# Window attention on TensorE: one head per tile of the array, and one score tile for a pair of windows

## The chip, the cores and the metric

The kernel runs on one NeuronCore of a Trainium2 chip, as a single launch. The metric is the device time of that launch in microseconds; the core's own time is the kernel's time. The kernel before takes 12572.97 us, the median of three runs (12561.93, 12572.97 and 12574.42).

## What is computed

A network of four layers works on images `x` of 4 x 256 x 64 x 64 (batch, channels, rows, columns), in fp32. Each layer adds to `x` what it makes of its group-normalised input. Layers 0 and 1 are attention layers, layers 2 and 3 are Mamba layers (a recurrence along 4096 positions); the change touches the attention layers alone. In such a layer, for each of the 4 images:

- `y` comes from a gated recurrence along one axis, after four 1x1 convolutions with tanh and sigmoid.
- `y` is cut into 8 x 8 windows of 64 positions. `q`, `k` and `v` are linear in `y` (256 to 3 x 256).
- For each window, the mean `q` is compared with the mean `k` of all 64 windows, and the 4 best windows are chosen.
- The window's 64 queries attend to the 4 x 64 = 256 positions of the chosen windows, in 8 heads of 32 channels:

```python
attn = softmax(einsum('bphqd,bphkd->bphqk', qh * SCALE, kh))
out = einsum('bphqk,bphkd->bphqd', attn, vh)
```

- `out` plus a depthwise 3x3 convolution of `v` ("lepe" in the code) goes through a last linear map `wo`.

## The kernel before

For each batch the kernel does layer 0, layer 1, layer 2 and layer 3 one after the other. `attention_layers` does both attention layers of a batch; its order of work is written out by hand, so each engine executes its instructions in the order of the source, and only waits on semaphores shift them against the other engines. A tile that is allocated again under the same tag waits for those that used the buffer before; `bufs` says how many buffers a tag has.

A layer has two phases. `scan_phase` goes over 8 strips of 8 columns and produces `y`, the keys and values (written to DRAM by window, `kvd`) and the value image `vimg`. `window_phase` then goes over 32 pairs of windows, `for i in range(n_pair)` (L620 on), and is software-pipelined: iteration `i` issues the scores, least values and exponentials of pair `i + 1` and the transposes and values of pair `i`. The steps:

- `gather` (L455 on): loads the keys and values of the four chosen windows into `kv`, 128 rows for two of the chosen windows and two such halves (`j`) along the free axis.
- `queries` (L257 on): two 1x1 convolutions per strip make `q` for 8 windows; ScalarE writes it to `qbuf` (L266), and two DMAs copy each half of it to the other 64 partitions (`double`, L275). `qbuf` holds two heads beside each other, `[P, 2, NW, 2, 64]`, and has zeros where a row belongs to the other head; they are written once, at the start of the program (L105).
- `scores` (L480): for each of the two windows `w`, a matmul has 64 rows (two heads of 32 channels), 128 columns (two heads x 64 queries, block diagonal because of the zeros) and 128 key positions. Row half `r` holds different keys. That is 16 matmuls per pair. The result is `sc[w]`, a PSUM tile of 128 x 1024 for each window, with two buffers.
- `smallest` (L491): VectorE reduces `sc[w]` to the least value of each query and head, once for each window (the scores carry the opposite sign, so this is the softmax's maximum).
- `exps` (L502): ScalarE takes the exponentials, 4 instructions of 128 x 256 per window, each with the sum of its rows; it issues them in halves, `(0, 1)` and `(2, 3)`, around the copies of `turned`.
- `normalise`: VectorE takes the reciprocal of the sums (L512), and POOL multiplies (L514, 128 x 1024).
- `turn` (L528): TensorE transposes the attention weights, 8 transposes per window; `turned` copies them to SBUF, half by VectorE (L539) and half by ScalarE (L541).
- `values` (L552): 8 matmuls per window with 128 rows (key positions), 64 columns (the channels of two heads) and 128 moving columns (the queries of both heads). Half of what they write belongs to the wrong head. The result is `ov`, one buffer.
- `own_rows` (L565): VectorE adds the four useful quarters of `ov` to `vimg`, 32 partitions each.

Between these, the loop runs a convolution per pair in most iterations (`queries` for a later strip or `project`, the map `wo` of an earlier one, both L208; `add` at L577 is the sum that follows the latter), `taps` on POOL (the depthwise convolution of the last two strips, L229, L230 and L242), and the steps of the next group norm, planned in `mids` (after the first `smallest`) and `ends` (at the end of an iteration): sums L149, means L155, centring L157, squares L165, sums of squares L169.

fp32 matmuls appear in the trace as two instructions each, so that the 16 matmuls of a pair's scores are 32 rows of L480; transposes appear as one.

Of the kernel before, what the change touches and what calls it, by code (L numbers as in the profile page):

```python
# [24 lines left out]
NH = 4  # L25
# [20 lines left out]
class Net:  # L46
# [33 lines left out]
    def attention_layers(self, x, w_drams, v_drams):  # L80
        tc, nc = self.tc, self.nc
        with ExitStack() as ctx:
# [17 lines left out]
                [big.tile([P, 2, NW, 2, 64], F32, name=f"q{i}{m}") for m in range(2)]  # L100
                for i in range(2)
            ]
            for t in qbuf[0] + qbuf[1]:
                for r in range(0, P, 32):
                    nc.gpsimd.memset(t[r : r + 32, :, :, 1 - r // 32 % 2, :], 0.0)  # L105
# [151 lines left out]
            def queries(lay, s, m, psum):  # L257
# [4 lines left out]
                def evict():  # L262
                    for h in range(NH):
                        rows = slice(h * 32, h * 32 + 32)
                        b, h2 = divmod(h, 2)
                        nc.scalar.activation(  # L266
                            q[rows, b, :, h2, :].rearrange("p w (j i) -> p w j i", i=8),
# [166 lines left out]
            def window_phase(lay, work, psum, idx, nxt):  # L434
# [31 lines left out]
                sc = {}  # L466
# [3 lines left out]
                def scores(i):  # L470
                    sj, a = divmod(i, 4)
                    for w in range(2 if i < n_pair else 0):
                        sc[w] = psum.tile([P, 2, 4, P], F32, tag="sc", name="sc", bufs=2)
                        t = kv[i, w]
                        for cq in range(4):
                            m, b = divmod(cq, 2)
                            for r in range(2):
                                rows = slice(r * 64, r * 64 + 64)
                                k0 = b * P + m * 64
                                nc.tensor.matmul(  # L480
                                    sc[w][:, r, cq, :],
                                    qbuf[sj % 2][m][rows, b, 2 * a + w].rearrange("p h t -> p (h t)"),
                                    t[rows, :, k0 : k0 + 64], start=True, stop=True,
                                )

                mn = {}

                def smallest(i, w):
                    if i < n_pair:
                        mn[w] = self.small.tile([P, 4], F32, tag="mn", name="mn", bufs=4)  # L490
                        nc.vector.tensor_reduce(  # L491
                            mn[w], sc[w].rearrange("p r c n -> p c r n"), AX.XY, ALU.min
                        )

                def exps(i, w, part=range(4)):
                    if i < n_pair:
# [4 lines left out]
                        for cq in part:  # L501
                            nc.scalar.activation(  # L502
# [1494 lines left out]
```

## Time and profile before

| | us |
|---|---|
| median of three runs | 12572.97 |
| the profiled execution, its own time | 12578.04 |
| span of its instructions | 12576.3 |
| busy in the span: PE / DVE / POOL / ACT | 10378.1 / 10244.0 / 9022.1 / 7241.3 |
| L480 scores, matmuls (8192 rows), union of their times | 575.6 |
| L552 values, matmuls (8192 rows), union of their times | 595.9 |
| L491 least values (512) | 610.0 |
| L565 own rows (1024, 418 ns each) | about 428 |
| L266 queries to SBUF (512, median 680 ns each) | about 348 |
| first scores to last values, first window phase | 226.7 to 509.0 |
| first scores to last values, second window phase | 709.5 to 1006.2 |

How to read it: the profile is one execution. "Busy" is the time in which an engine has work in flight; matmuls overlap each other, so a matmul's own duration (289 ns for L480) is longer than the distance to the next one. The name in front of a line number is the engine; `x2048` is a count; the shapes are partitions x elements. After the bar stand the busy time, the mean of one in ns, and the time the engine sat idle before such instructions, with what ended it. In a timeline the first number is the start in us, the second the length of a run of like instructions. The mean granted clock of TensorE over the span is 0.915 of full speed.

### The profile page before, as it was taken

The page shows a single profiled execution, that of the slowest core. Times are in us where ns is not written, and L with a number is a line of the kernel's source. Part 1 is how long each engine was busy: PE and PEld are TensorE (multiplying, and loading weights), DVE is VectorE, ACT ScalarE, POOL GpSimd, SP SyncE. Part 2 cuts the span into 40 slices and gives each one's busy share as a digit, 9 for nine tenths or more (in the row PEclk, how much of TensorE's full clock was granted, in tenths as well). Part 3 has the DMA queues.
Part 4 walks back from the last instruction along what each step waited for, and adds up shares of the span by engine and source line. Part 5 has one row for each costly group of instructions (what it writes and reads, how often), then busy time and mean ns, then how long its engine had stood idle before and what let it go on. Part 6 is the DMA issues. An engine that isn't in the chain of part 4 may idle for free. (4 is left out here: it accounts for less than half of the span.)

```text
span 12576.3 us, 159645 instructions
## 1 busy us (share of the span) xinstructions
PE 10378.1 (83%) x54656; PEld 6079.4 (48%) x54656; DVE 10244.0 (81%) x9074; ACT 7241.3 (58%) x13292; POOL 9022.1 (72%) x4634
## 2 busy tenths in 40 slices
PE   8987887777898788778789878877778987887787
PEld 4664444443466454444446645444434664444443
DVE  6778997887677899798767789978976778997897
ACT  4565554776456555477646655547764565554776
POOL 4666886887466688688746668868874666886887
PEclk9998998998899899899889989989988998998998
DMA  3343444554334455455433445445543344554554
GB/s 96 106 130 129 171 168 137 168 169 141 98 107 126 132 169 169 137 170 169 141 98 108 127 133 170 168 137 169 169 141 97 107 128 131 171 168 138 169 168 142
DMA packets 687147, 1782.94 MB, mean 142 GB/s; under 512 B 89856, under 2 KB 197888, under 8 KB 685312
## 3 DMA queue, kind: packets, MB, share of 16 engines
q1 hardware_dynamic: 686336, 1772.74, 43.6%
q8 instruction: 435, 7.13, 0.2%
q14 instruction: 376, 3.08, 0.1%
HBM read 1610.91 MB, written 94.37 MB: 136 GB/s over the span
## 5 line engine op out<-in xcount | busy, mean ns | idle before, releaser
L925 POOL TENSOR_TENSOR hc<-h,cb 128x1024 f32<-128x1024 f32 x2056 | 4817.5, 2351 | 1099.0 <-DVE h L919 502.8
L919 DVE TENSOR_TENSOR_SCAN h<-da,m_state,pb 128x1024 f32<-128x1024 f32 x1248 | 2920.4, 2340 | 162.0 <-DVE pb L913 1.9
L872 PE MATMUL y<-ident,hc 128*128 128x128 f32 x16384 | 2378.0, 294 | 313.7 <-POOL hc L925 211.4
L872 PEld LDWEIGHTS y<-ident,hc 128*128 128x128 f32 x16384 | 2098.8, 152 | 979.4 <-POOL hc L925 374.5
L913 DVE TENSOR_TENSOR pb<-du,pb 128x1024 f32<-128x1024 f32 x1672 | 2025.8, 1212 | 147.3 <-PE pb L844 98.8
L856 ACT ACTIVATE da<-delta,m_v 128x1024 f32<-128x1024 f32 x1672 | 1899.1, 1141 | 215.9 <-DVE h L919 205.4
L844 PE MATMUL pb<-m_parts,pick 128*128 128x512 bf16 x3280 | 1082.2, 414 | 896.9 <-DVE h L919 893.7
L502 ACT ACTIVATE pr<-sc,mn 128x256 f32<-128x256 f32 x2048 | 956.7, 478 | 783.9 <-PE pt_ps L528 560.7
L514 POOL TENSOR_TENSOR pr<-pr,sm 128x1024 f32<-128x1024 f32 x512 | 967.8, 1896 | 572.3 <-DVE sm L512 392.4
L844 PEld LDWEIGHTS <-pick 128*128 128x128 bf16 x3280 | 253.0, 101 | 1884.2 <-DVE h L919 1226.5
L919 DVE TENSOR_TENSOR_SCAN h<-da,pb 128x1024 f32<-128x1024 f32 x424 | 969.7, 2287 | 55.5 <-DVE pb L913 1.4
L830 POOL TENSOR_TENSOR bb<-du,bb 128x1024 f32<-128x1024 f32 x376 | 888.7, 2363 | 71.8 <-DMA bb<-m_cd 65.2
L491 DVE TENSOR_REDUCE mn<-sc 128x4 f32<-128x1024 f32 x512 | 610.0, 1219 | 257.4 <-PE sc L480 256.0
L919 DVE TENSOR_TENSOR_SCAN h<-dap,m_state,bb 128x1024 f32<-128x1024 f32 x288 | 672.1, 2334 | 80.4 <-ACT dap L856 67.7
L528 PE MATMUL pt_ps<-ident,pr 128*128 128x128 f32 x4096 | 572.3, 283 | 144.5 <-ACT pts L541 64.2
L208 PE MATMUL conv_ps<-att_y,att_wb 128*128 128x512 f32 x1536 | 688.8, 593 | 0.0
L856 ACT ACTIVATE dap<-delta,m_v 128x1024 f32<-128x1024 f32 x376 | 419.6, 1116 | 457.7 <-DVE h L919 349.1
L552 PE MATMUL ov_ps<-pts,kv 128*64 128x128 f32 x8192 | 595.9, 294 | 91.1 <-DVE vimg L565 74.6
L480 PE MATMUL sc<-kv,q 64*128 64x128 f32 x8192 | 575.6, 289 | 81.4 <-DMA kv<-kv_dram 58.6
L528 PEld LDWEIGHTS pt_ps<-ident,pr 128*128 128x128 f32 x4096 | 466.5, 144 | 314.1 <-issue 152.2
L480 PEld LDWEIGHTS sc<-kv,q 64*128 64x128 f32 x8192 | 518.3, 197 | 124.6 <-issue 46.5
L552 PEld LDWEIGHTS ov_ps<-pts,kv 128*64 128x64 f32 x8192 | 468.1, 144 | 216.3 <-DVE vimg L565 131.1
(263 smaller groups left out, 18265.0 us busy)
## 6 DMA issues: line engine op xcount, KB each, us to landing
cb<-m_cd SPq DMA_DIRECT2D x2048, 512.0 KB, 3.8
kv<-kv_dram SPq DMA_DIRECT2D x2048, 128.0 KB, 2.6
bb<-m_cd SPq DMA_DIRECT2D x376, 512.0 KB, 5.1
q<-q SPq DMA_DIRECT2D x256, 256.0 KB, 3.9
kv_dram<-kst SPq DMA_DIRECT2D x128, 256.0 KB, 3.5
kv_dram<-vn SPq DMA_DIRECT2D x128, 256.0 KB, 3.6
x<-in_x_dram SPq DMA_DIRECT2D x8, 2048.0 KB, 10.7
m_pe<-in_pe_dram SPq DMA_DIRECT2D x32, 512.0 KB, 5.2
```

The costliest lines, as they stand in the source:

```text
L480: nc.tensor.matmul(sc[w][:, r, cq, :], qbuf[sj % 2][m][rows, b, 2 * a + w].rearrange("p h t -> p (h t)"), t[rows, :, k0 : k0 + 64], start= ...
L502: nc.scalar.activation(t[:, cq].rearrange("p j r t -> p r j t"), sc[w][:, :, cq, :].rearrange("p r (j t) -> p r j t", j=2), AF.Exp, bias=m ...
L514: nc.gpsimd.tensor_tensor(t, t, s.rearrange("p (a o) -> p a o", o=1).to_broadcast([P, 4, 256]), ALU.mult,)
L528: nc.tensor.transpose(pt[w][j][:, cq, :], t[:, cq, j].rearrange("p r t -> p (r t)"), self.ident,)
L552: nc.tensor.matmul(ov[i][b * 64 : b * 64 + 64, m, :, :, w, :], t[:, j, c0 : c0 + 64], pts[w][j][:, cq, :], start=(j == 0), stop=(j == 1),)
L830: nc.gpsimd.tensor_tensor(pb[i], slots[i][0]["du"], pb[i], ALU.mult)
L844: nc.tensor.matmul(pb[i][:, ss], self.pick[:, n : n + 1].to_broadcast([P, P]), blk["parts"][:, ss], start=True, stop=True,)
L856: nc.scalar.activation(da[i], blk["delta"], AF.Exp, scale=blk["a"](n))
L872: nc.tensor.matmul(blk["y"][:, ss], t[:, ss], self.ident, is_transpose=True, start=(n == 0 and ss.start % NT == 0), stop=(n == DS - 1 and ...
L913: nc.vector.tensor_tensor(pb[i], blk["du"], pb[i], ALU.mult)
L919: nc.vector.tensor_tensor_scan(h[i][:, ss], da[i][:, ss], pb[i][:, ss], state, ALU.mult, ALU.add)
L925: nc.gpsimd.tensor_tensor(hc[i][:, ss], h[i][:, ss], cb[i][:, ss], ALU.mult)
```

## The change

The array is used in smaller tiles, one head per matmul.

- `qbuf` loses the axis with two heads, and the zeroing at the start goes. `evict` writes 64 partitions in one instruction, 2 instructions in place of 4.
- `scores` has 32 rows (one head) and 64 columns (its queries) per matmul: 32 matmuls per pair in place of 16, on 8 tiles of the array (4 row positions x 2 column positions). Both windows go to one PSUM tile `sc[i]` of 128 x 2048, with one buffer.
- `smallest` reduces both windows at once.
- `exps` reads its parts at other places of `sc[i]`; number and shape stay.
- `values` has 32 columns (one head's channels) and 64 moving columns: 32 matmuls per pair in place of 16, on 4 column tiles. `ov` is half as large.
- `own_rows` becomes one instruction on 128 partitions.
- In the loop, one `smallest(i + 1)` follows `scores(i + 1)`; the second call, which came after `turn(i, 0)` and `mids`, is gone.

```diff
-                [big.tile([P, 2, NW, 2, 64], F32, name=f"q{i}{m}") for m in range(2)]
+                [big.tile([P, 2, NW, 64], F32, name=f"q{i}{m}") for m in range(2)]
                 for i in range(2)
             ]
-            for t in qbuf[0] + qbuf[1]:
-                for r in range(0, P, 32):
-                    nc.gpsimd.memset(t[r : r + 32, :, :, 1 - r // 32 % 2, :], 0.0)
...
                 def evict():
-                    for h in range(NH):
-                        rows = slice(h * 32, h * 32 + 32)
-                        b, h2 = divmod(h, 2)
+                    for b in range(2):
+                        rows = slice(b * 64, b * 64 + 64)
                         nc.scalar.activation(
-                            q[rows, b, :, h2, :].rearrange("p w (j i) -> p w j i", i=8),
+                            q[rows, b].rearrange("p w (j i) -> p w j i", i=8),
...
                 def scores(i):
                     sj, a = divmod(i, 4)
-                    for w in range(2 if i < n_pair else 0):
-                        sc[w] = psum.tile([P, 2, 4, P], F32, tag="sc", name="sc", bufs=2)
-                        t = kv[i, w]
-                        for cq in range(4):
-                            m, b = divmod(cq, 2)
-                            for r in range(2):
-                                rows = slice(r * 64, r * 64 + 64)
-                                k0 = b * P + m * 64
-                                nc.tensor.matmul(
-                                    sc[w][:, r, cq, :],
-                                    qbuf[sj % 2][m][rows, b, 2 * a + w].rearrange("p h t -> p (h t)"),
-                                    t[rows, :, k0 : k0 + 64], start=True, stop=True,
-                                )
...
                     if i < n_pair:
+                        sc[i] = psum.tile([P, 2, 2, 2, 2, P], F32, tag="sc", name="sc", bufs=1)
+                        for w in range(2):
+                            for m in range(2):
+                                for r in range(2):
+                                    for h in range(2):
+                                        r0 = r * 64 + h * 32
+                                        rows = slice(r0, r0 + 32)
+                                        for b in range(2):
+                                            k0 = b * P + m * 64
+                                            nc.tensor.matmul(
+                                                sc[i][b * 64 : b * 64 + 64, r, h, w, m, :],
+                                                qbuf[sj % 2][m][rows, b, 2 * a + w],
+                                                kv[i, w][rows, :, k0 : k0 + 64],
+                                                start=True, stop=True,
+                                            )
...
+                def smallest(i):
+                    if i < n_pair:
+                        mn[i] = self.small.tile([P, 8], F32, tag="mn", name="mn", bufs=4)
                         nc.vector.tensor_reduce(
-                            mn[w], sc[w].rearrange("p r c n -> p c r n"), AX.XY, ALU.min
+                            mn[i].rearrange("p (g h) -> p g h", h=2),
+                            sc[i].rearrange("p r h w m n -> p (w m) h r n"), AX.XY, ALU.min,
                         )
...
                         for cq in part:
+                            m, h = divmod(cq, 2)
                             nc.scalar.activation(
                                 t[:, cq].rearrange("p j r t -> p r j t"),
-                                sc[w][:, :, cq, :].rearrange("p r (j t) -> p r j t", j=2),
-                                AF.Exp, bias=mn[w][:, cq : cq + 1], scale=-1.0,
+                                sc[i][:, :, h, w, m, :].rearrange("p r (j t) -> p r j t", j=2),
+                                AF.Exp, bias=mn[i][:, w * 4 + cq : w * 4 + cq + 1], scale=-1.0,
...
                 def values(i, w):
                     if w == 0:
-                        ov[i] = psum.tile([P, 2, 2, 8, 2, 8], F32, tag="ov", name="ov_ps", bufs=1)
+                        ov[i] = psum.tile([P, 2, 8, 2, 8], F32, tag="ov", name="ov_ps", bufs=1)
...
                             for b in range(2):
-                                cq = 2 * m + b
-                                c0 = C + cq * 64
-                                nc.tensor.matmul(
-                                    ov[i][b * 64 : b * 64 + 64, m, :, :, w, :],
-                                    t[:, j, c0 : c0 + 64], pts[w][j][:, cq, :],
-                                    start=(j == 0), stop=(j == 1),
-                                )
+                                for h in range(2):
+                                    p0 = b * 64 + h * 32
+                                    c0 = C + m * P + p0
+                                    nc.tensor.matmul(
+                                        ov[i][p0 : p0 + 32, m, :, w, :], t[:, j, c0 : c0 + 32],
+                                        pts[w][j][:, 2 * m + h, b * 64 : b * 64 + 64],
+                                        start=(j == 0), stop=(j == 1),
+                                    )
...
-                        for r in range(4):
-                            rows = slice(r * 32, r * 32 + 32)
-                            out = vimg[rows, :, 8 * sj : 8 * sj + 8, 1 + a * 16 : 17 + a * 16]
-                            nc.vector.tensor_tensor(
-                                out, ov[i][rows, :, r % 2].rearrange("p m j w i -> p m j (w i)"),
-                                out, ALU.add,
-                            )
-                        del ov[i]
+                        out = vimg[:, :, 8 * sj : 8 * sj + 8, 1 + a * 16 : 17 + a * 16]
+                        nc.vector.tensor_tensor(
+                            out, ov.pop(i).rearrange("p m j w i -> p m j (w i)"), out, ALU.add
+                        )
...
                 scores(0)
+                smallest(0)
                 for w in range(2):
-                    smallest(0, w)
                     exps(0, w)
                     normalise(0, w)
...
                     scores(i + 1)
-                    smallest(i + 1, 0)
+                    smallest(i + 1)
                     for t in mids.get(i, ()):
                         t()
                     turn(i, 0)
-                    smallest(i + 1, 1)
                     exps(i + 1, 0, (0, 1))
```

More of the change, by code (lines that the diff above doesn't have):

```diff
@@ L24 @@
 NW = 8
-NH = 4
 TOPK = 4
@@ L464, in gather @@
                                 )
[L466 removed]
+                sc, mn = {}, {}
                 def scores(i):
                     sj, a = divmod(i, 4)
[L472 to L484 removed]
@@ L486, in window_phase @@
-                mn = {}
-                def smallest(i, w):
-                    if i < n_pair:
-                        mn[w] = self.small.tile([P, 4], F32, tag="mn", name="mn", bufs=4)
+                    if i < n_pair:
+                        sc[i] = psum.tile([P, 2, 2, 2, 2, P], F32, tag="sc", name="sc", bufs=1)
[13 more added lines that the diff above has]
+                                            )
```

## The prediction

> **What bounds the kernel now.** I read the page first, for the share of each engine and the groups that the diff touches:
>
> ```profile
> PE 10378.1 (83%) x54656; PEld 6079.4 (48%) x54656; DVE 10244.0 (81%) x9074; ACT 7241.3 (58%) x13292; POOL 9022.1 (72%) x4634
> ...
> L502 ACT ACTIVATE pr<-sc,mn 128x256 f32<-128x256 f32 x2048 | 956.7, 478 | 783.9 <-PE pt_ps L528 560.7
> L514 POOL TENSOR_TENSOR pr<-pr,sm 128x1024 f32<-128x1024 f32 x512 | 967.8, 1896 | 572.3 <-DVE sm L512 392.4
> ...
> L491 DVE TENSOR_REDUCE mn<-sc 128x4 f32<-128x1024 f32 x512 | 610.0, 1219 | 257.4 <-PE sc L480 256.0
> ...
> L552 PE MATMUL ov_ps<-pts,kv 128*64 128x128 f32 x8192 | 595.9, 294 | 91.1 <-DVE vimg L565 74.6
> L480 PE MATMUL sc<-kv,q 64*128 64x128 f32 x8192 | 575.6, 289 | 81.4 <-DMA kv<-kv_dram 58.6
> ```
>
> The shares average over the whole network and the chain that ended last lies in the later layers, so neither decides. The counts do: L502 runs 8 times per pair of windows, so there are 256 pairs, 32 in each of 8 window phases (4 batches x 2 layers). From the first score to the last value they last 282 to 286 us in the first layer and 297 in the second, some 2,320 of 12,576 us. Nothing outside them changes by more than a few us.
>
> Then the timeline of one pair in mid-phase (start, length, engine, line):
>
> ```profile
> 407.80 2.75 ACT L266 ACTIVATE q<-conv_ps,neg_bq 32x512 f32<-32x512 f32 x4
> 407.88 2.06 PE L480 MATMUL sc<-kv,q 64*128 64x128 f32 x32
> ...
> 409.09 2.35 DVE L491 TENSOR_REDUCE mn<-sc 128x4 f32<-128x1024 f32 x2 [0.87 <-PE sc L480]
> ...
> 409.86 1.09 PE L528 MATMUL pt_ps<-ident,pr 128*128 128x128 f32 x8
> ...
> 410.79 1.88 PE L208 MATMUL conv_ps<-att_y,att_wb 128*128 128x512 f32 x4
> 411.04 0.47 ACT L502 ACTIVATE pr<-sc,mn 128x256 f32<-128x256 f32 x1 [0.49 <-PE pt_ps L528]
> ...
> 411.96 1.71 DVE L565 TENSOR_TENSOR vimg<-ov_ps,vimg 32x256 f32<-32x256 f32 x4
> ...
> 413.72 2.35 PE L552 MATMUL ov_ps<-pts,kv 128*64 128x128 f32 x32 [0.17 <-DVE vimg L565]
> ...
> 415.48 0.49 ACT L502 ACTIVATE pr<-sc,mn 128x256 f32<-128x256 f32 x1
> 415.84 0.22 ACT L502 ACTIVATION_READ_ACCUMULATOR pr<-sc,mn 128x1 f32 x1
> 415.93 2.75 ACT L266 ACTIVATE q<-conv_ps,neg_bq 32x512 f32<-32x512 f32 x4
> 416.00 1.86 PEld L480 LDWEIGHTS sc<-kv,q 64*128 64x128 f32 x32 [0.17 <-issue]
> ```
>
> L480 returns every 8.12 us, and TensorE is occupied nearly throughout: **PE's own order of work sets the pair.** The last `exp` of the pair ends at 416.06, after the next scores have begun; two `sc` tiles let them overlap.
>
> **What the change does to this chain.** Scores, least value and `exp`s of a pair now share one `sc` tile (`bufs=1`, as large as the two before). Scores of the next pair can't start before ScalarE has read the last `exp` of this one. That closes a loop over three engines, in which none works ahead. Its terms:
>
> 1. Last accumulator read to first weight load: 0.05 (51 ns where L480 waited for ScalarE now).
> 2. Scores. The trace doesn't show eight tiles at once. Now the 16 instructions of one window run on two row tiles in eight rounds of 112 ns, the two starts of a round 7 ns apart, 1.16 from first load to last end. After: 64 instructions on eight tiles (4 row x 2 column), again eight per tile. Eight tiles 7 ns apart add 0.04; 64-column loads (L552) have rounds of 109. I take 1.15. Below 1.12 it can't go: that is one tile's own eight. The upper bound is the present pace, a load and a matmul per 56 ns: 64 x 0.056 + 0.27 = 3.85. I choose the low end, since in each round two matmuls already start 7 ns apart and the third waits for its own tile.
> 3. PE to VectorE: 0.05.
> 4. One reduction of 2048 elements: 128x512 takes 0.67 (L308), 128x1024 1.22, so two more steps of 0.55: 2.30 (bounds 2.2 and the two it replaces, 2.36).
> 5. VectorE to ScalarE: 0.10.
> 6. Eight `exp`s and two copies: a block of exp-exp-copy-exp-exp starts 2.30 after the one before where nothing holds it (747.06 to 749.36), and ends 2.42 after its start: 4.72. The held block today starts at 413.64 because the second turn ends at 413.55; in the loop that turn ends 2.31 after the first `exp`, so it holds nothing.
>
> Sum 0.05+1.15+0.05+2.30+0.10+4.72 = **8.37 us, against 8.12: +0.25 per steady pair.** So the quicker matmuls are paid for by the lost overlap.
>
> A rule weighed. Row: two tiles' matmuls start 7 ns apart. The Trainium skill, TensorEngine Tiling (Array Packing), section Performance Considerations, Instruction Overhead, puts about 60 cycles on every matmul and warns against tiling a dimension that is already small. At the 2.4 GHz that its page TensorE: Matmul & The Clock Gate gives in its head table, that is 25 ns; 64 would take 1.6 us, an estimate from these two pages, and the loop would be 8.8. The 7 ns of this trace speak against it for different tiles, but only for two.
>
> **What else changes inside the pair.** It all falls off the path:
> - Values: 64 instructions, half as many columns, four column tiles instead of two. By the same rounds 0.7 us per window with its tail, now about 1.1. Bounds: 0.5, and 32 x 0.056 + 0.27 = 2.1. They end about 8.1 into the loop, under the last `exp`s; with the upper bound they would add about 1.
> - L565: four operations of 0.42 on 32 partitions become one on 128. ScalarE's 32x512 (0.68) and 128x512 (0.69) show that partitions cost nothing, so 0.42. It saves VectorE 1.3 per pair, which had kept values waiting ([0.17 <-DVE vimg]); the late thing there becomes the copies of the turned tiles.
> - L266: four of 0.68 become two; 1.38 saved, hidden under scores and reduction. The q copies move half the bytes, three pairs ahead of use. The 15.7 us of zeroing at the start end 1.0 after VectorE's mean is ready: -1.0 once.
> - POOL needs 2 x 1.89 + 4/3 x 2.83 = 7.55 per pair, with a 2.47 every fourth pair of the second layer 8.2: still under 8.37, but with little room.
>
> **Pairs that stall today gain.** In the second layer every fourth pair takes 11 to 12.3 us. Its cause:
>
> ```profile
> 834.51 1.23 DVE L491 TENSOR_REDUCE mn<-sc 128x4 f32<-128x1024 f32 x1 [0.88 <-PE sc L480]
> 837.16 1.22 DVE L169 TENSOR_REDUCE gn_s<-att_xn 128x4 f32<-128x1024 f32 x1 [1.43 <-ACT att_xn L165]
> 838.30 1.21 DVE L491 TENSOR_REDUCE mn<-sc 128x4 f32<-128x1024 f32 x1
> ```
>
> The statistics' reduction stands between the two least values and waits for a square that waits for the 2.75 eviction; everything behind is late, and PE drops to half clock for 3.4 us. After, one L491 goes ahead of it and the eviction is half as long. What is late next is the first copy (1.14 behind the reduction), then the second block by 0.6: 8.97.
>
> **The sum for one batch** (start-to-start intervals of L480, from the timeline):
> - 22 steady pairs of the first layer and 10 of the second, +0.25 each: +8.0.
> - The other 17 intervals of the second layer: 158.2 now. After: five with the reduction 8.97, five beside them with column sums 8.6, two where two taps and the 2.47 meet on POOL 10.25, five 8.6 to 8.4: 150.9. -7.3.
> - Last five intervals of the first layer, 47.0, bound by POOL's queue: -1.2.
> - Phase start: both windows' scores before the first `exp`, which pushes eight taps of VectorE (8.3 us) and the next L491 back: +1.0 each, +2.0. The third interval is 7.86 now, no convolution in it, 8.37 after: +1.0 for two. Pairs without convolution leave PE 2 us idle and may meet half clock (0.5 granted at 258.5 today): +1.0.
> - Tails: -0.3 and, with L565 between values and the last projection, -2.5: -2.8.
> - Four evictions fewer beside each of two strips in the scan phase: -1.0.
>
> 8.0-7.3-1.2+2.0+1.0+1.0-2.8-1.0 = -0.3; four batches -1.2, zeroing -1.0: **-2 us.** The profiled execution took 12578.0 (span 12576.3), 5 above the median, so 12578 - 2 stands for a median of 12571. Its own error: 0.15 per steady pair (32 x 4 x 0.15 = 19), as much for the stalled ones, 12 for starts: about 40.
>
> **Rivals.**
> 1. *The tiles don't run eight at a time* (slower). Place: term 2, decisive from about 1.5 us on. If four overlap, 16 rounds make it 2.05, +0.9 per pair, x 248 = +223: 12,795. At the present pace +2.7, +670: 13,240. Half clock in a third of the pairs would add 1 to those, +80: 12,650. For it: no more than two tiles are ever shown together, and PE is emptier. Against: the 7 ns, and that PE is still busy some 6 us of 8.4.
> 2. *The waits are finer than the tile* (faster). If the first window's scores start as soon as its own `exp`s are through, about half of term 2 leaves the loop: 7.8 per pair, 0.55 x 46 x 4 = 100 less: 12,470. Against: today the second window's first load waits for ScalarE as a whole tile would; and both windows now lie interleaved in one tile.
> 3. *It doesn't do what it says*: a reduction through strides or eviction over 64 partitions slower than its row. 0.3 on term 4 is +75: 12,645.
>
> **How the numbers follow.** Forecast 55%, of which 0.15 below, 0.27 within and 0.13 above 0.2% (25 us, about what a measurement of this kernel can tell from no change). Rival 1 20%, slower; rival 3 8%, slower or same; rival 2 17%, faster. Faster 0.15 + 0.17 = 0.32, same 0.27 + 0.02 = 0.29, slower 0.39. The forecast's own range is 12,530 to 12,610; the given one, 12,470 to 12,700, leaves out four overlapping tiles and worse, and little below.
>
> **What would show it.** Right: L480 starts 0.05 after L502's last read in nearly every steady pair, its run is 1.15, L491 x256 takes 2.30, L565 x256 0.42, the period is 8.37, and PE's idle time before L480 is put down to L502. Wrong: an L480 run above 1.5 (rival 1), L480 starting before L502 has ended (rival 2), L491 above 2.4 (rival 3), or a granted clock in the window phases clearly below the 0.94 to 0.96 of now. If the period is right and the total is not, the stalled pairs were mis-sized.

## The result, and the profile after

The changed kernel takes 12635.21 us (median of 5 runs, 12622.74 to 12641.08), the kernel before 12572.97 (5 runs on the same chip): a ratio of 1.0051, 95% interval 1.0040 to 1.0062. So it is 0.5% slower, about 62 us, where the forecast was 2 us less. The profiled execution took 12630.46 us; its span is 52.4 us longer than that of the profile before.

The page of the changed kernel, head and groups (busy time, mean of one in ns, idle time before them and its main releaser):

```profile
span 12628.7 us, 191060 instructions
...
PE 10051.6 (80%) x71040; PEld 5667.3 (45%) x71040; DVE 9883.3 (78%) x8050; ACT 7057.2 (56%) x13036; POOL 8962.5 (71%) x4570
...
L502 ACT ACTIVATE pr<-sc,mn 128x256 f32<-128x256 f32 x2048 | 954.3, 478 | 995.6 <-DVE mn L489 678.1
L514 POOL TENSOR_TENSOR pr<-pr,sm 128x1024 f32<-128x1024 f32 x512 | 968.2, 1896 | 632.9 <-DVE sm L512 356.6
L489 DVE TENSOR_REDUCE mn<-sc 128x8 f32<-128x2048 f32 x256 | 586.6, 2291 | 285.1 <-PE sc L478 284.8
L554 PE MATMUL ov_ps<-pts,kv 128*32 128x64 f32 x16384 | 400.7, 235 | 183.7 <-ACT pts L541 95.6
L478 PE MATMUL sc<-kv,q 32*64 32x128 f32 x16384 | 365.6, 298 | 186.2 <-ACT pr L502 107.7
```

Every engine is busy for less time than before, PE by 327 us, and the kernel is slower. The right-hand column says why: scores now wait for ScalarE's exponentials (L478, released by `pr` L502), the reduction waits for the scores (L489, by `sc`), and the exponentials wait for the reduction (L502, by `mn` L489: 678 us; before, most of that idle time was put down to the turned tile, `pt_ps`). That is a ring of waits, each engine idle while another works.

One pair of the changed kernel in the timeline (start, length, engine, line):

```profile
407.65 0.22 ACT L502 ACTIVATION_READ_ACCUMULATOR pr<-sc,mn 128x1 f32 x1
...
407.93 1.26 PE L478 MATMUL sc<-kv,q 32*64 32x128 f32 x64 [0.37 <-ACT pr L502]
...
409.24 2.29 DVE L489 TENSOR_REDUCE mn<-sc 128x8 f32<-128x2048 f32 x1 [1.09 <-PE sc L478]
...
411.65 0.47 ACT L502 ACTIVATE pr<-sc,mn 128x256 f32<-128x256 f32 x1 [3.77 <-DVE mn L489]
412.05 0.41 DVE L564 TENSOR_TENSOR vimg<-ov_ps,vimg 128x256 f32<-128x256 f32 x1
...
413.80 0.65 PE L554 MATMUL ov_ps<-pts,kv 128*32 128x64 f32 x32
...
416.17 0.22 ACT L502 ACTIVATION_READ_ACCUMULATOR pr<-sc,mn 128x1 f32 x1
...
416.44 1.26 PE L478 MATMUL sc<-kv,q 32*64 32x128 f32 x64 [0.37 <-ACT pr L502]
```

From 407.93 to 416.44 is 8.51 us, the steady period; before it was 8.12. ScalarE stands idle for 3.77 us in each pair (behind the bracket of 411.65), and that is scores, reduction and the gaps between.

Where the time came from, by classes of start-to-start intervals of the scores (sum per batch, mean of the four batches, from the timeline):

| | predicted | measured |
|---|---|---|
| steady intervals, 22 + 10 | +8.0 | +13.5 |
| first four intervals of both phases | +4.0 | +6.2 |
| last five of the first layer | -1.2 | +1.8 |
| other 17 of the second layer | -7.3 | -3.9 |
| tails | -2.8 | +1.0 |
| sum, eight phases: times 4 | +0.7: +3 | +18.6: +74 |
| rest of the program | -5 | -22 |

The classes go by the scores' start: "tails" run from a phase's last scores to the end of its last values, so what stands behind the last values counts as the rest of the program.

### The profile page after: what moved, and what is told of

It reads as the page before. It is cut to its first block, busy times and chain, and to the rows that moved or that the text cites. A ratio compares the mean times of both kernels' runs of the same rounds, so it can differ in the third digit from the quotient of the medians.

```text
span 12628.7 us, 191060 instructions
## 1 busy us (share of the span) xinstructions
PE 10051.6 (80%) x71040; PEld 5667.3 (45%) x71040; DVE 9883.3 (78%) x8050; ACT 7057.2 (56%) x13036; POOL 8962.5 (71%) x4570
## 4 chain that ended last, share of the span: by engine, by line
DVE 19%; PE 18%; ACT 11%; issue 4%; POOL 3%; DMA 1%; DVEq 0%; SPq 0%; ACTq 0%; POOLq 0%
DVE h L915 9%; DVE pb L909 4%; PE conv_ps L204 4%; PE y L868 3%; ACT pr L502 3%; PE u_ps L1200 2%; DVE mn L489 1%; ACT da L852 1%; PE pb L840 1%; PE sc L478 1%; DVE lp L240 1%; PE u_ps L1566 1%; ACT pts L541 1%; POOL hc L921 1%; ACT dap L852 1%
## 5 line engine op out<-in xcount | busy, mean ns | idle before, releaser
L502 ACT ACTIVATE pr<-sc,mn 128x256 f32<-128x256 f32 x2048 | 954.3, 478 | 995.6 <-DVE mn L489 678.1
L528 PE MATMUL pt_ps<-ident,pr 128*128 128x128 f32 x4096 | 639.4, 297 | 256.3 <-DVE pts L539 132.4
L489 DVE TENSOR_REDUCE mn<-sc 128x8 f32<-128x2048 f32 x256 | 586.6, 2291 | 285.1 <-PE sc L478 284.8
L512 DVE RECIPROCAL sm<-sm 128x4 f32<-128x4 f32 x512 | 91.0, 178 | 722.0 <-ACT pr L502 612.0
L554 PE MATMUL ov_ps<-pts,kv 128*32 128x64 f32 x16384 | 400.7, 235 | 183.7 <-ACT pts L541 95.6
L478 PE MATMUL sc<-kv,q 32*64 32x128 f32 x16384 | 365.6, 298 | 186.2 <-ACT pr L502 107.7
L240 DVE SCALAR_TENSOR_TENSOR lp<-vimg,att_v,lp 128x512 f32<-128x512 f32 x616 | 465.5, 756 | 28.3 <-DVE lp L240 1.0
```

Source lines behind the costliest of these rows:

```text
L489: nc.vector.tensor_reduce(mn[i].rearrange("p (g h) -> p g h", h=2), sc[i].rearrange("p r h w m n -> p (w m) h r n"), AX.XY, ALU.min,)
L502: nc.scalar.activation(t[:, cq].rearrange("p j r t -> p r j t"), sc[i][:, :, h, w, m, :].rearrange("p r (j t) -> p r j t", j=2), AF.Exp, b ...
L528: nc.tensor.transpose(pt[w][j][:, cq, :], t[:, cq, j].rearrange("p r t -> p (r t)"), self.ident,)
```

## Experiments

The theory at the start: the single score tile closes a loop over PE, VectorE and ScalarE, and each term of it shows in the pair. Rivals: the small matmuls or half clock on PE set the pair; or something else does (POOL, the `mm` buffer, the copies of the turned tiles). All times are medians; each ratio is to runs of the kernel before on the same chip, with its 95% interval.

### The parts of the change alone

**values_only**: the kernel before with the new `values` and `own_rows`, nothing else (their diff is in the section on the change, but for the moving operand, since two heads still lie beside each other).

```diff
+                                        pts[w][j][:, 2 * m + b, h * 64 : h * 64 + 64],
```

> The kernel before with the new values and the single own_rows alone: 32 columns per head, no other edit. Before, PE's own order sets the pair (8.12 us) and the values are 2.35 us of it, with a wait for own_rows. In the changed kernel they run 0.65 per window. If PE's order is what counts, the pair gets up to 1 shorter, until POOL (7.55 per pair) or ScalarE (4.74 + 2.75 = 7.5 in pairs with an eviction) is the bound: 7.6 to 7.8 per steady pair, 32 x 4 x -0.4 = -51, tails some -10, the stalled pairs a little: about 12,500 us. Rival: small matmuls cost what wide ones do, and the pair stays at 8.1: 12,560 to 12,575.

Measured: 12495.35 us, ratio 0.9943 (0.9929 to 0.9956). The time is as expected, the way only in part: the steady pairs go from 8.12 to 8.03 (mean of 7.8, 8.4 and 8.0 in turn), less than thought, and the stalled pairs from 12.3 to 10.3. So the small values are a gain by themselves, where PE's order still sets the pair.

**scores_only**: the changed kernel with `values` and `own_rows` of before.

```diff
-                                    p0 = b * 64 + h * 32
-                                    c0 = C + m * P + p0
+                                cq = 2 * m + b
+                                c0 = C + cq * 64
...
+                                    t[:, j, c0 : c0 + 64], pts[w][j][:, cq, :],
```

> The changed kernel with the values and the four own_rows of before; the 64 columns of a values matmul are then channels of two other heads than those whose weights it takes, so its output is not the reference's, while counts, sizes and waits are those of before. If the loop over the one score tile (8.51) sets the pair and the values lie beside it, the steady pair stays near 8.5 and only the tails and the longer own_rows add: 12,650 to 12,680. Rival: the loop is not the bound and the quicker values earned something in it: then 2 x 0.5 come back per pair, 9.3, 12,635 + 230 = 12,860.

Measured: 12646.24 us, ratio 1.0063 (1.0049 to 1.0077); steady period 8.51, the same as with the small values. So inside the loop the same edit that is worth 74 us to the kernel before is worth 11 to 15 (by the times and by the ratios). In the steady pairs it was placed rightly "off the path".

**one_tile**: the kernel before with one tile, one buffer, and a joint reduction.

```diff
-                        sc[w] = psum.tile([P, 2, 4, P], F32, tag="sc", name="sc", bufs=2)
+                        sc[i] = psum.tile([P, 2, 2, 4, P], F32, tag="sc", name="sc", bufs=1)
...
-                    smallest(i + 1, 0)
+                    smallest(i + 1)
...
-                    smallest(i + 1, 1)
```

> The kernel before with the two score tiles joined to one with one buffer and one joint reduction; its wide matmuls, zeros and values stay. It tells what the lost overlap alone costs. Theory: the same loop with the old scores: 0.05 + 2.06 + 0.06 + 2.29 + 0.12 + 4.74 = 9.3 per steady pair in place of 8.12, with the stalled pairs of the second layer about 2 shorter: (1.2 x 27 + 1.2 x 22 - 2 x 5) x 4 = +195: 12,765. Rival: PE's order, not the tile, sets the pair: 8.1 to 8.5, 12,570 to 12,650.

Measured: 12868.05 us, ratio 1.0236 (1.0220 to 1.0251), some 100 more than expected: the pairs that were to shrink did not (the 17 intervals rose by 14 per batch, and the starts, the last five and the tails by 20 together). The steady period is the expected one. Its timeline:

```profile
416.60 0.22 ACT L504 ACTIVATION_READ_ACCUMULATOR pr<-sc,mn 128x1 f32 x1
...
416.87 2.12 PE L481 MATMUL sc<-kv,q 64*128 64x128 f32 x32
...
419.03 2.29 DVE L492 TENSOR_REDUCE mn<-sc 128x8 f32<-128x2048 f32 x1 [1.94 <-PE sc L481]
...
421.44 0.47 ACT L504 ACTIVATE pr<-sc,mn 128x256 f32<-128x256 f32 x1 [4.62 <-DVE mn L492]
```

The same ring, with 2.12 for the scores; the period is 9.36. So the lost overlap costs 299 us, the quicker scores, together with the halved evictions of `q`, return some 220 of them (12868 to 12646), and the quicker values 11 to 15.

### The terms of the loop

**four_tiles**: the changed kernel, with another order of its matmuls.

```diff
-                        for w in range(2):
-                            for m in range(2):
-                                for r in range(2):
-                                    for h in range(2):
+                        for h in range(2):
+                            for w in range(2):
+                                for m in range(2):
+                                    for r in range(2):
```

> The changed kernel with the matmuls of a pair's scores in another order, h outermost, so that only four of the eight tiles of the array are used at a time; all else is the same. Theory (every term of the loop shows in the pair): scores take 16 rounds of 109 ns and some 0.3, 2.05 in place of 1.26, the steady pair 9.3, and +0.78 x 250 = +195: 12,830. Rival: the loop is not what sets the pair, and PE has 2 us to spare: 12,640 to 12,680.

Measured: 12764.49 us, ratio 1.0152 (1.0137 to 1.0168), 129 above the changed kernel. Its scores in the timeline:

```profile
410.27 1.71 PE L478 MATMUL sc<-kv,q 32*64 32x128 f32 x64 [0.37 <-ACT pr L502]
...
419.24 1.72 PE L478 MATMUL sc<-kv,q 32*64 32x128 f32 x64 [0.37 <-ACT pr L502]
```

The run is 1.72, not 2.05, and the period 8.97: 0.46 more in the run, 0.46 more in the pair. PE has idle time, and none of it takes this up. The rival is out.

**split**: the changed kernel, with a least value per window in the places of before.

```diff
-                            sc[i].rearrange("p r h w m n -> p (w m) h r n"), AX.XY, ALU.min,
+                            sc[i][:, :, :, w].rearrange("p r h m n -> p m h r n"), AX.XY, ALU.min,
...
-                    smallest(i + 1)
+                    smallest(i + 1, 0)
...
                     turn(i, 0)
+                    smallest(i + 1, 1)
```

> The changed kernel with the least values taken by window again, 128x1024 each, in the two places of before; scores, tile and values as changed. Theory: the one tile closes a loop, and the 2.29 reduction is a term of it. With 1.22 in its place the loop is 8.51 - 1.07 = 7.44, and POOL (7.55) or a few waits come next: 7.6 to 7.8 per steady pair, -0.8 x 32 x 4 = -100, and the pairs with group norm steps shed some of their 9.2 too: 12,480 to 12,530. Rival A, the small scores on PE or half clock set the pair: no change, 12,620 to 12,645. Rival B, the first copy and the second turn behind the second reduction set it, as they are where they were before: about 8.1, 12,580.

Measured: 12643.33 us, ratio 1.0060 (1.0046 to 1.0074): nothing gained, against my theory's 100 us. Its timeline says where the gain stayed:

```profile
411.41 2.36 DVE L489 TENSOR_REDUCE mn<-sc 128x4 f32<-128x1024 f32 x2 [1.07 <-PE sc L478]
...
413.88 0.47 ACT L502 ACTIVATE pr<-sc,mn 128x256 f32<-128x256 f32 x1 [3.84 <-DVE mn L489]
```

The first `exp` of window 0 needs only the first reduction, and yet begins 0.12 after the second has ended. In 243 of the 256 pairs that distance is 0.12, in five it is longer, and only in the first pair of each phase, whose steps are issued in another order, is the `exp` ahead. Before, the first `exp` began 0.40 ahead of that end. What differs is where a window lies: before in a tile and two banks of its own, now in one tile with the other, with half of each of the four banks. (Banks are the parts that PSUM, the memory of the matmuls' results, is made of.) The Trainium skill, PSUM — Partial Sum Buffer, section "PSUM bank collisions raise a hardware error", says that the compiler back end keeps accesses of two engines to one bank and 32-partition quadrant apart by an added dependency, two reads too; this trace agrees with its 0.12. No run separates the shared bank from the shared tile. The theory of the loop stands (with 2.36 for both reductions it sums to 8.59, and the period is 8.58), but cutting the reduction by window doesn't open it. Cutting the tile by head does.

**by_head**: two tiles of two banks, one for `h = 0` and one for `h = 1`, each with both windows.

```diff
-                        sc[i] = psum.tile([P, 2, 2, 2, 2, P], F32, tag="sc", name="sc", bufs=1)
-                        for w in range(2):
-                            for m in range(2):
-                                for r in range(2):
-                                    for h in range(2):
+                        for h in range(2):
+                            sc[i, h] = psum.tile([P, 2, 2, 2, P], F32, tag="sc", name="sc", bufs=2)
+                            for w in range(2):
+                                for m in range(2):
+                                    for r in range(2):
...
-                    smallest(i + 1)
+                    smallest(i + 1, 0)
...
+                    smallest(i + 1, 1)
-                    exps(i + 1, 0, (0, 1))
+                    exps(i + 1, 0, (0, 2))
```

> The changed kernel with the score tile cut by head: two tiles of two banks each (h = 0 and h = 1, both windows in each), the matmuls of h = 0 ahead of those of h = 1, one 128x1024 least value per tile, and in each window the exps of h = 0 first. In the split by window the first exp began 117 ns after the second reduction in all but 8 of 256 pairs: both windows lie in all four banks, so its exps waited for both reductions and the loop stayed at 8.6. Theory (the one tile closes the loop): with no bank shared, scores of h = 0 start 1.5 before the last exp and their reduction lies beside them; ScalarE's 4.74 and about 1 are left of the loop, which binds no more. POOL (7.55) and the order on PE come next, as in the kernel before with the new values (7.8 to 8.4): 7.6 to 8.0 per steady pair, 12,470 to 12,510, with four tiles at a time on PE in place of eight. Rival A, small scores or half clock on PE set the pair: 8.5 or more, 12,630 to 12,700. Rival B, the waits stay on the whole pair however the tile is cut: as split, 12,643.

Measured: 12490.27 us, ratio 0.9944 (0.9930 to 0.9958), as the theory had it. Its timeline:

```profile
417.35 0.48 ACT L501 ACTIVATE pr<-sc,mn 128x256 f32<-128x256 f32 x1
...
417.54 1.62 PE L478 MATMUL sc<-kv,q 32*64 32x128 f32 x64
...
418.70 2.36 DVE L489 TENSOR_REDUCE mn<-sc 128x4 f32<-128x1024 f32 x2 [0.50 <-PE sc L478]
...
420.26 0.47 ACT L501 ACTIVATE pr<-sc,mn 128x256 f32<-128x256 f32 x1 [2.34 <-POOL pr L513]
```

Scores begin while the last `exp` still runs, the reduction before the scores have ended, and the first `exp` 0.80 before the second reduction ends. It is now put down to POOL, which frees the `pr` buffer. Most steady intervals are 7.5, with an 8.7 here and there (mean of the first layer's 22: 7.81): the loop is open, although only four tiles of the array work at a time. But the ratio is that of values_only (0.9943), which has the wide scores of before: with the loop open, the small scores neither cost nor earn anything that these times can tell, and the gain over the kernel before is no more than that of the new values.

**copies_dve**: the loop shortened on ScalarE's side.

```diff
-                        nc.scalar.activation(pts[w][1], pt[w][1], AF.Copy)
+                        nc.vector.tensor_copy(pts[w][1], pt[w][1])
```

> The changed kernel with the second half of each turned tile copied by VectorE in place of ScalarE; scores, tile and joint reduction as changed. It shortens the loop from another side: two copies of 0.59 leave ScalarE's 4.74. Theory (period = scores run + 7.25, as in three kernels: 8.51 - 1.26, 8.98 - 1.72, 9.36 - 2.12): the loop is 8.51 - 1.18 = 7.33 and binds no more where POOL (7.55, two taps in every third pair) is longer; VectorE has 4 x 0.69 of copies and 2.29 and stays under it: 7.5 to 8.0 per steady pair, 12,480 to 12,530. Rival: the copies now queue behind the reduction and the second turn comes late, so the exps wait for the turned tile: 8.3 to 8.6, 12,600 to 12,640.

Measured: 12488.31 us, ratio 0.9936 (0.9922 to 0.9950). The common interval is 7.67. The expectation took 0.59 off for each copy; eight `exp`s one behind the other, 0.45 to 0.53 apart, still take 3.82 from the first to the end of the last read.

With that, one sum holds for five kernels (gap, scores, gap, reduction, gap, exps to the last read, medians over all pairs; the period is the median of the first layer's 22 steady intervals):

| | sum | its value | period |
|---|---|---|---|
| changed | 0.05+1.26+0.06+2.29+0.12+4.74 | 8.52 | 8.51 |
| split | 0.05+1.26+0.06+2.36+0.12+4.74 | 8.59 | 8.58 |
| four_tiles | 0.05+1.72+0.07+2.29+0.12+4.73 | 8.98 | 8.97 |
| one_tile | 0.05+2.13+0.04+2.29+0.12+4.74 | 9.37 | 9.36 |
| copies_dve | 0.13+1.26+0.06+2.29+0.12+3.82 | 7.68 | 7.67 |

That the parts of a ring add up to its period is arithmetic; what the table shows is that the gaps between them stay at 0.04 to 0.13 in all five, so that no engine has slack in the loop.

### The pairs with group norm steps

In the changed kernel the intervals of 12.3 in the second layer are 9.0, but their neighbours of 8.1 to 8.5 have become 9.2. A pair of this kind, from the end of the first layer's phase, where the same steps run:

```profile
469.08 2.29 DVE L489 TENSOR_REDUCE mn<-sc 128x8 f32<-128x2048 f32 x1 [1.33 <-PE sc L478]
...
471.29 0.16 DVE L151 COPY gn_mean<-gn_pm 128x8 f32<-128x8 f32 x1
...
471.50 1.99 PE L204 MATMUL conv_ps<-vimg,att_wb 128*128 128x512 f32 x4 [1.45 <-DVE gn_mean L151]
...
474.45 0.48 ACT L502 ACTIVATE pr<-sc,mn 128x256 f32<-128x256 f32 x1 [0.54 <-PE pt_ps L528]
```

The copy of the mean (L151, in `mids`) stands behind the whole reduction, where before only the first half was ahead of it. It frees the single `mm` buffer, so the convolution starts 1.45 late; the second turn stands behind that on PE, and ScalarE waits 0.54 for the buffer. The same wait of the convolution shows 40 times in this profile, 20 of them for the copy of the mean (29.0 us in all) and 20 for that of the variance (L172, 30.8 us); in the profile before it shows not once.

**mids_first**: all of `mids` ahead of the reduction.

```diff
-                    smallest(i + 1)
                     for t in mids.get(i, ()):
                         t()
+                    smallest(i + 1)
```

> The changed kernel with the planned group norm steps in mids moved ahead of the joint reduction. Theory for the pairs that became 9.2: the small statistics copy stands behind the 2.29 reduction and holds the one mm buffer, so the pair's convolution waits 1.45 for it. Moved ahead, the convolution has its buffer in time: 9.2 goes to 8.6 in some 12 pairs of a second-layer phase, and less in the last five of a first-layer phase: -0.6 x 12 x 4 - 1 x 4 = -33, 12,600. Rival: the 9.2 come from half clock or from POOL and not from the buffer: no change, 12,625 to 12,640; or the steps that go ahead hold up the reduction, which is in the loop: slower by their length, 0.3 x 60 = +18.

Measured: 12633.83 us, ratio 1.0050 (1.0036 to 1.0063). No change in the sum, but both halves of the story are in the intervals. Of the two 9.2 for each stalled pair, the one with the copy of the mean became 8.5 (with one exception in 16); the one with the copy of the variance, right behind the stalled pair, became 8.75 in 9 of 16 cases and 9.5 or more in the others. The pairs with the statistics' own reduction, which goes ahead as well, rose from 9.0 to about 11.2.

**copies_first**: the two small copies ahead, that reduction behind (the first edit in both plans, `gn` and `stats`).

```diff
-                             (ends, i + 2), (mids, i + 3), (ends, i + 3), (mids, i + 4))
+                             (ends, i + 2), (lates, i + 3), (ends, i + 3), (mids, i + 4))
...
-                    smallest(i + 1)
                     for t in mids.get(i, ()):
                         t()
+                    smallest(i + 1)
+                    for t in lates.get(i, ()):
+                        t()
```

> The changed kernel with the small statistics copies (mean, variance) ahead of the joint reduction and the statistics' reduction behind it. With all three moved ahead, the pairs of 9.2 went to 8.5 to 8.8 as expected of the one mm buffer, and the pairs with the statistics' reduction went from 9.0 to 11.2, which ate the gain. Theory: now both are had, 9.2 goes to 8.6 in some 9 pairs of a second-layer phase, the 9.0 stay, and the first-layer phases lose 3.5 as they did: (-0.6 x 9 - 3.5) x 4 = -36, about 12,600. Rival: the 9.0 pairs grow by what their neighbours lose: 12,625 to 12,640.

Measured: 12595.57 us, ratio 1.0021 (1.0012 to 1.0030), 40 below the changed kernel. The 17 intervals sum to 150.7, the first layer's last five to 47.2, its tail to 13.3. The 9.2 are 8.5 and 8.75, the 9.0 stay, and no convolution waits for a small copy any more. The pair shown above, in this kernel:

```profile
467.27 0.17 DVE L151 COPY gn_mean<-gn_pm 128x8 f32<-128x8 f32 x1
...
468.48 2.29 DVE L489 TENSOR_REDUCE mn<-sc 128x8 f32<-128x2048 f32 x1 [1.04 <-PE sc L478]
...
469.28 1.88 PE L204 MATMUL conv_ps<-vimg,att_wb 128*128 128x512 f32 x4
```

The copy is ahead of the reduction, and the convolution runs beside it.

**values_late** and **by_head_late**: the same move of the statistics' reduction behind the second least value (`lates` after `smallest(i + 1, 1)`), on values_only and on by_head.

```diff
+                    for t in lates.get(i, ()):
+                        t()
                     exps(i + 1, 0, (0, 1))
```

> The kernel before with the new values alone, and the statistics' reduction moved behind the second least value. The same question on the order of before: its stalled pairs are 10.3 (four a second-layer phase). Theory: 10.3 goes to about 9, -1.3 x 4 x 4 = -21, 12,475. Rival: no change, 12,490 to 12,500.

> The kernel with the score tile cut by head, and the statistics' reduction moved behind the second least value. Theory: what is left of the stall is the reduction between the two least values (pairs of 11.4, three a second-layer phase, and 9.4); behind them it delays only the first copy: 11.4 goes to 9, the 9.4 beside them stay or lose a little: -2.4 x 3 x 4 = -29, 12,460. Rival: POOL or the eviction sets those pairs: 12,485 to 12,500.

Measured: values_late 12479.06 us, ratio 0.9928 (0.9913 to 0.9942), with intervals of 9.2 to 9.4 in place of 10.3; and by_head_late 12486.93, ratio 0.9935 (0.9921 to 0.9949), 3 less than by_head, which this measurement can't tell from nothing: the intervals of 11.4 stayed, the 9.4 became 8.4. So in the order of before the statistics' reduction between the two least values does cost something, as the prediction said: about 1.0 us in such a pair by the intervals; the total times of values_late and values_only are too close to tell. In by_head the 11.4 have another cause, which was not followed up.

**mended**: the changed kernel with the edits of copies_dve and of copies_first.

> The changed kernel with both halves of each turned tile copied by VectorE and with the small statistics copies ahead of the joint reduction, the statistics' reduction behind it: the two edits that helped it, together. With the copies by VectorE alone, steady pairs took 7.7 and the pairs with group norm steps 9.2, 9.2, 8.7 in turn. Theory: the 9.2 come from the small copy behind the reduction, which holds the one mm buffer and so the convolution, and they go to about 8.2 as the same move took 0.6 from them in the slower loop; 10 pairs per second-layer phase and 2 per first-layer phase: -0.8 x 12 x 4 = -38, 12,450. Rival: VectorE is the bound in those pairs, since it has the copies now: 12,480 to 12,495.

Measured: 12474.22 us, ratio 0.9923 (0.9909 to 0.9937), the lowest of all, by 14 below copies_dve rather than 38: of the sequence 9.2, 9.2, 8.7 the first stayed and the others became 8.8 and 8.4. mended, values_late, by_head_late, copies_dve, by_head and values_only lie within some 21 us of each other, and each interval overlaps the others. All beat both kernels.

## Why the prediction was wrong

The mechanism of the loop was right, but the small copies of the group norm were left out of the path; the value 12,571 was 64 us low, and the change is slower by more than the 0.2% that separates it from none. The forecast's own range, 12,530 to 12,610, missed the time. The given range held it only because it was widened for three rivals, none of which came true; and in the profiled executions the window phases were forecast 71 us too short, of which the rest of the program gave 17 back by savings of which only a part is explained. Point by point:

- **The loop.** All six terms were the right ones, and the rival of waits finer than the tile didn't come true. Term 2 was mis-sized: 1.26, not 1.15. The records don't name the tile, but by the order of the starts in one pair the first four tiles start 0, 6, 13 and 20 ns after the first matmul, and the other four 160 to 180 ns after it, not 28 to 49 as "eight tiles 7 ns apart" has it; the 64 starts reach over 0.99 us. The trace of before had a hint that the prediction passed over: its rounds are not 112 ns apart throughout, the second starts 213 ns after the first in 228 of 256 pairs. The exps' term was 4.74 for 4.72. Together the period is 8.51 for 8.37, and the steady pairs cost +13.5 per batch for +8.0: 22 us over four batches.
- **The rule weighed.** The estimate from the Trainium skill's 60 cycles (TensorEngine Tiling (Array Packing), Instruction Overhead) was 1.6 us for the run and 8.8 for the loop. Measured are 1.26 and 8.51: neither the rule nor my reading of the 7 ns, but nearer to the latter. The mean distance of two successive starts is 15.7 ns.
- **Reduction, L565, evictions, values.** 2.29 (2.30), 0.41 (0.42), 0.68 for 64 partitions, and 0.65 for a window's values (0.7): right. The values and L565 are off the path of the steady pairs, as scores_only shows.
- **Pairs with group norm steps: the step that failed.** The pairs with the statistics' reduction itself came to 8.97, as forecast ("What is late next is the first copy"). What failed is the price of their neighbours, put at 8.4 to 8.6 and measured at 9.2. There the small statistics copies, which stood behind one half reduction, stand behind the whole one, and they free the one `mm` buffer that the pair's convolution needs; the prediction put this wait at nothing, and it is 1.5 us of the convolution, 40 times. The 17 intervals came to 154.6 for 150.9. With the copies ahead of the reduction (copies_first) they are 150.7, and the first layer's last five and its tail fall by 1.6 and 1.7 too. I had counted what is queued behind the waiting reduction on its engine, but not which buffer the queued instruction gives back. That is 26 of the missing us over four batches by these classes (1.6 + 1.7 + 3.9, less 0.6 by which the second layer's tail is longer, times 4), and some 40 by the time of copies_first.
- **Tails.** -2.8 was forecast, +1.0 came: +1.5 in the first layer, which copies_first takes back, and -0.5 for -2.5 in the second. The shorter L565 did show in the second layer, but behind the last values, where this table counts it with the rest of the program. The last projection waits for it, here at the end of the second batch's phase, before and after:

```profile
4160.39 1.98 PE L208 MATMUL conv_ps<-vimg,att_wb 128*128 128x512 f32 x4 [2.01 <-DVE vimg L565]
...
4180.58 1.98 PE L204 MATMUL conv_ps<-vimg,att_wb 128*128 128x512 f32 x4 [0.59 <-DVE vimg L564]
```

  That is 1.4 us less in each batch.
- **Starts and clock.** +6.2 for +4.0. The indicator that I named, a granted clock clearly below 0.94 to 0.96, came true: 0.90 and 0.92 in the first two window phases, 0.94 in the same stretches before. Two stretches of the first phase (length, busy times of PE, PEld, DVE, ACT and POOL, then PEclk, the granted clock):

```profile
300.00:400.00 100.00, 78.79 (x1739) 50.94 (x1742) 56.50 (x78) 64.27 (x228) 82.73 (x54) 1.00 0.49 140
400.00:500.00 100.00, 77.35 (x1671) 53.20 (x1658) 56.01 (x77) 59.27 (x208) 84.20 (x52) 0.91 0.46 132
```

  In mid-phase the clock is full, so half clock is no part of the steady 8.51; from 400 to 500, where the last pairs have gaps on PE, it is 0.91 (0.98 before). In the last 50 us of the four first-layer phases the clock is at half for 20 to 24 us, before for 3 to 10, and in copies_first for 10 to 14. So part of what the copies cost at the ends of these phases may be the clock that followed. How much of the starts and ends is clock was not separated.
- **The rest of the program** came out 22 shorter for 5. Its code is the same but for the evictions of q, the zeroing and the last L565 of a phase. 12 of the 22 lie between the first batch's last values and the second batch's first scores, where the later batches gain 3 to 4. Of the 12, 4 are the end of that phase: 1.4 by L565, and 2.6 because its last projections ran at a lower granted clock in the profile before (0.62 from 1008 to 1017; 2.92 and 3.67 us for the 1.98 of other batches). The first scores start at 226.7 in both profiles, so the 1.0 for the zeroing didn't come. The cause of the remainder stays open.

## What to carry to other kernels

A faster operation that needs a larger buffer must be priced with the buffer: here some 220 us of quicker matmuls didn't pay for 299 us of lost overlap. With the tile cut so that the reduction of one half and the exponentials of the other share neither tile nor bank, the small matmuls showed no cost, but with the new values in both they didn't beat the wide ones either (0.9944 and 0.9943). When an instruction moves behind a longer one on its engine, ask not only who waits for its result, but which buffer its end gives back, and to whom. A loop over several engines without a second buffer is a sum: add its terms, and what shortens or lengthens one of them shows in the period (0.46 of 0.46 in four_tiles, 0.84 of 0.92 in copies_dve), until the next bound.

## What the hardware showed that was not expected

- The 64 instructions of 32 small matmuls on eight tiles of the array take 1.26 us from first load to last end; in an order that uses four tiles at a time, 1.72; the 32 instructions of the 16 wide ones of before, in the loop of one_tile, 2.12. Twice the tiles gave 1.37 times the speed, not twice.
- The run on eight tiles doesn't fill them evenly: by the order of the starts, the second four tiles begin 160 ns behind the first four (in 219 of 256 pairs; 270 ns in most of the others), and a tile's own starts lie some 110 to 130 ns apart.
